# Attention of a Perceiver layer: eight TensorE runs per group become six, with seven rotating PSUM banks

## The chip, the cores and the metric

The kernel runs on one core of a Trainium2 chip. The metric is the device time of one launch in microseconds (us); a smaller number is better. The core has five engines that run side by side and wait for each other through semaphores: TensorE (PE in the profile; PEld is its loading of weights), VectorE (DVE), ScalarE (ACT), GpSimd (POOL) and SyncE (SP), which here issues most DMAs. TensorE writes its results to PSUM, which has eight banks, each of 512 float32 values on 128 partitions. The other memory on the core is SBUF.

## The reference

The layer has three parts, each added to the residual x of 16 batches, 64 rows and 1024 features, in float32. The change is to the first, cross attention:

```python
xq = layernorm(x).reshape(b, s, 8, 4, 32)      # 8 groups of 4 heads, 32 wide, 64 rows
xk = xv = ctx.reshape(b, 1601, 8, 32)          # keys and values are the same 1601 rows
scores = einsum("bsgrd,btgd->bgrst", xq, xk) / sqrt(32) + mask
out = einsum("bgrst,btgd->bsgrd", softmax(scores), xv)
x = x + out
```

The second part is a gated feed-forward layer (1024 to 2752) that zeroes the smaller half of its activations in each row; the third is a mixture of eight small experts of which each row uses two. The mask is one table of 64 x 1601 numbers that all batches share.

## The kernel before

**Groups.** Attention is cut into 64 groups: a batch, one half (`h`) of the eight key-value heads, and one half (`rh`) of the four query heads that share each of them. A group holds four key-value heads `g`, each with 2 x 64 = 128 rows of queries, so its scores are four tables of 128 x 1601.

**What one group goes through** (class `Group`, lines 235 to 358):

- `scores(c)`: TensorE multiplies queries and keys. The contraction is 32 long, so four heads occupy four strips of 32 rows of the array and run at once. The 1601 keys are cut into four parts (`PARTS`, line 29) of 289, 512, 288 and 512. One call is one part of all four heads: four matmuls, which show as eight rows, since float32 takes two passes. The 512 parts are called long here, the others short.
- `masked(c)`: VectorE reads each head's part from PSUM, adds the mask, writes it to SBUF (`sc`) and keeps the row maximum (`mx`). After the last part it reduces the maxima to `nm`.
- `softmax(g)`: ScalarE takes the exponential of one head's 1601 columns in place and sums it.
- `turn(heads)`: TensorE transposes two heads' exponentials in blocks of 128 columns, 26 transposes, four to a PSUM bank: three banks for each head and one that holds the last 65 columns of both. Eight copies take them to SBUF (`pT`): the first five by ScalarE, the sixth and the two small ones by VectorE.
- `values(c0, c1)`: TensorE multiplies the transposed blocks with the values. Each output is 32 wide, so the four heads use four strips of 32 columns and run at once. All 13 blocks accumulate in one bank, `po`, in two calls of 6 and 7 blocks.
- `keep()`: ScalarE copies `po` to `oT`; VectorE takes the reciprocals of the sums. When all groups of two batches are done, `finish_tile` transposes `oT` back and GpSimd scales it and adds it to x.

**The order.** Every engine works off its instructions in the order in which the program lists them (`InOrder`, lines 85 to 98). The loop of lines 418 to 484 goes over the groups n; each turn has two halves d. TensorE's order in a half is: a long score run of group n+1; in some halves the turning of later queries (`turn_queries`) or of finished results (`finish_tile`); the transposes of two heads of group n; a short score run of group n+1 (d = 0) or n+2 (d = 1); half of the values of group n-1. So there are four runs in a half and eight in a group. VectorE's order is: four long masks, copies 6 to 8, four short masks, and in the second half the reciprocals. ScalarE's is: five copies, two exponentials, and in the second half the copy of `po`. Scores and masks are thus half a group ahead of the loop, and six calls of `scores` stand ahead of it (line 407).

**PSUM.** One bank is `po`'s (`ps_o`). Three are for scores of heads 0 to 2 (`ps_s`). Four rotate (`ps_t`) among the scores of head 3, the transposes and the turned queries and results. A tile that is given a bank waits until all that used the tile before it in that bank is done.

**DMA.** `load_kv(b)` loads keys and values of a batch on SP's queue; it is called from `scores(0)` of the second group of the batch before. For the first batch the keys come in the four `PARTS`, each with two copies of its mask columns, in twelve DMAs. GpSimd in the meantime prepares sums of the feed-forward weights, one piece in each turn of the loop (`sums_in`, `sums_made`, `sums_out`).

**After attention** the feed-forward and expert parts run in an order that a planner (class `Plan`) works out from written costs and ranks. The last group's values and `keep` are its first tasks (lines 1239 and 1240).

Of the kernel before, what the change touches and what calls it, by code (L numbers as in the profile page):

```python
# [9 lines left out]
F32 = mybir.dt.float32  # L10
# [6 lines left out]
ALU = mybir.AluOpType  # L17
AX = mybir.AxisListType
PSUM = bass.MemoryType.PSUM

P = 128
B, S, D = 16, 64, 1024
T, C = 1601, 256
HD = 32
NT = B * S // P
NTC = (T + P - 1) // P
TL = T - (NTC - 1) * P

PARTS = [(0, 289), (289, 801), (801, 1089), (1089, T)]
NCH = len(PARTS)  # L30
I = 2752
IC = 344
NIC = I // IC
# [21 lines left out]
def tile_perceiver_layer(  # L55
# [22 lines left out]
    ident = const.tile([P, P], F32, name="ident")  # L78
# [18 lines left out]
    pe, dve, act = InOrder(nc.tensor), InOrder(nc.vector), InOrder(nc.scalar)  # L97
# [43 lines left out]
    otp = new_pool(late, "oT", 2, "right")  # L141
    twp = new_pool(early, "tw", 3)
    xp = new_pool(late, "x", 3, "right")
    ps_s = new_pool(early, "ps_s", 1, "left", PSUM)
    ps_t = new_pool(early, "ps_t", 4, "right", PSUM)

# [41 lines left out]
    def load_kv(b):  # L188
        kT = [ktp.tile([P, T], F32, tag="kT", name=f"kT{b}_{h}") for h in range(2)]
        v = [vp.tile([P, NTC, P], F32, tag="v", name=f"v{b}_{h}") for h in range(2)]  # L190
        full = (NTC - 1) * P
        for h in range(2):
            rows = ctx_t[b, h * P : (h + 1) * P]
            if b == h == 0:
                for t0, t1 in PARTS:
                    cols = slice(t0, t1)
                    sp_queue.dma_start(kT[h][:, cols], rows[:, cols])
                    for half in range(2):
                        sp_queue.dma_start(
                            mask2[half * S : (half + 1) * S, cols], mask[:, cols]  # L200
                        )
            else:
                sp_queue.dma_start(kT[h], rows)
        for h in range(2):
            cols = ctx_v[b, :, h * P : (h + 1) * P]
            sp_queue.dma_start(
                v[h][:, : NTC - 1, :], cols[:full].rearrange("(c p) d -> p c d", p=P)
            )
            sp_queue.dma_start(v[h][:TL, NTC - 1, :], cols[full:])
        kv[b] = kT, v  # L210
# [24 lines left out]
    class Group:  # L235
# [4 lines left out]
            self.name = f"{b}_{h}_{rh}"  # L240
            self.sc, self.pT = {}, {}

        def scores(self, c, spare=False):


            b, h, rh = self.b, self.h, self.rh
            if c == 0:
# [8 lines left out]
            t0, t1 = PARTS[c]  # L256
            homes = [[(ps_s, f"ps{g}"), (ps_t, "pt")] for g in range(3)]
            homes.append([(ps_t, "pt"), (ps_o, "po")])
            self.ps = []
            for g in range(4):  # L260
                home, tag = homes[g][spare]
                ps = home.tile([P, 512], F32, tag=tag, name=f"ps{g}_{self.name}_{c}")
                self.ps.append(ps)
            for g in range(4):
                rows = slice(g * HD, (g + 1) * HD)
                q = qT[b // 2][rows, h, b % 2, 2 * rh : 2 * rh + 2, :]
                pe.matmul(
                    self.ps[g][:, : t1 - t0],
                    q.rearrange("p r s -> p (r s)"),
                    kv[b][0][h][rows, t0:t1],  # L270
                    start=True,
                    stop=True,
                )

        def masked(self, c, heads=range(4)):


            t0, t1 = PARTS[c]
            for g in heads:
                dve.tensor_tensor_reduce(  # L280
                    out=self.sc[g][:, t0:t1],
                    in0=self.ps[g][:, : t1 - t0],
                    in1=mask2[:, t0:t1],
                    scale=1.0,
                    scalar=LOWEST,
                    op0=ALU.add,
                    op1=ALU.max,
                    accum_out=self.mx[:, g, c : c + 1],
                )
            if c == NCH - 1 and 2 in heads:  # L290
# [32 lines left out]
                )  # L323
            return copies

        def values(self, c0, c1):


            if c0 == 0:
                self.po = ps_o.tile([P, 512], F32, tag="po", name=f"po_{self.name}")  # L330
                self.po = self.po[:, :P]
            po, v = self.po, kv[self.b][1][self.h]
            for c in range(c0, c1):
                w = min(P, T - c * P)
                for g in range(4):
                    pe.matmul(
                        po[g * HD : (g + 1) * HD, :],
                        v[:w, c, g * HD : (g + 1) * HD],
                        self.pT[g][:w, c, :],
                        start=(c == 0),  # L340
                        stop=(c == NTC - 1),
                    )

        def keep(self):

            i, bb = self.b // 2, self.b % 2
            if bb == 0 and self.h == 0 and self.rh == 0:
                oT[i] = otp.tile([P, 2, 4, 2, S], F32, tag="oT", name=f"oT{i}")
                rs_tok[i] = small.tile([P, 2, 4, 4], F32, tag="rs", name=f"rs{i}")
            act.copy(  # L350
                oT[i][:, self.h, 2 * self.rh : 2 * self.rh + 2, bb, :],
                self.po.rearrange("p (r s) -> p r s", r=2),
            )
            for rl in range(2):
                dve.reciprocal(
                    rs_tok[i][bb * S : (bb + 1) * S, self.h, 2 * self.rh + rl, :],
                    self.sums[rl * S : (rl + 1) * S, :],
                )
# [35 lines left out]
    ng = len(groups)  # L394
# [9 lines left out]
        pe.transpose(warm[:, 0, :], ident, ident)  # L404
    for h in range(2):
        turn_queries(0, xn, h)
    for group, c in [(groups[0], c) for c in range(NCH)] + [(groups[1], c) for c in range(2)]:
        group.scores(c, spare=c % 2 == 1)
        if c % 2 == 0:
            for _ in range(4):  # L410
                pe.transpose(group.ps[3][:, 3 * P :], ident, ident)
        group.masked(c)
    for g in range(2):
        groups[0].softmax(g)

# [2 lines left out]
    for n in range(ng):  # L418
# [10 lines left out]
                sp_queue.dma_start(x[j], xs[j])  # L429
        for d in range(2):  # L430
            add = None
            long = (groups[n + 1], 2 * d + 1) if n + 1 < ng and n + d > 0 else None
            short = (groups[n + 1 + d], 2 - 2 * d) if n + 1 + d < ng else None
            if long:
                long[0].scores(long[1])
            if i < NT and d == 1 and m >= 6:
                turn_queries(i, xn, m - 6)
            if n > 8 and 3 <= 2 * m + d <= 4:
                copy, add = finish_tile(i - 2, 1 - d)
                act.copy(*copy)  # L440
            copies = group.turn((2 * d, 2 * d + 1))
            on_act = 3 if last else 5
            for copy in copies[:on_act]:
                act.copy(*copy)
            if long:
                long[0].masked(long[1], (3, 0, 1, 2))
            for copy in copies[on_act:]:
                dve.tensor_copy(*copy)
            if short:
                short[0].scores(short[1])  # L450
                short[0].masked(short[1])
            if d == 0:
                for g in (2, 3):
                    group.softmax(g)
            elif n + 1 < ng:
                for g in range(2):
                    groups[n + 1].softmax(g)
            if add:
                add()
            if n > 0:  # L460
                groups[n - 1].values(*((0, NTC // 2), (NTC // 2, NTC))[d])
                if d == 1:
                    groups[n - 1].keep()
            if i < NT:
                if (m, d) == (4, 0):
                    norm = Norm(x[i], f"q{i}")
# [769 lines left out]
    rank = {name: 10 + 10 * j for j, name in enumerate(order)}  # L1236
    gated = [gate(pairs[0], 0, rank["g0"], lambda i: [])]

    t = add("PE", 2.9, lambda: groups[-1].values(0, NTC), [], rank["g0"] - 5)
    t = add("ACT", 0.3, lambda: groups[-1].keep(), [t], 0)  # L1240

    def end():
        for h in range(2):
# [172 lines left out]
```

## Time and profile before

The median of three runs is 1718.9 us (1718.66 to 1722.92). The profiled execution has a span of 1719.5 us, 0.6 above the median.

| What | Value |
|---|---|
| Median of the runs | 1718.9 us |
| Profiled execution, first to last instruction | 1719.5 us |
| Busy over the span: TensorE, VectorE, ScalarE, GpSimd | 99%, 82%, 73%, 32% |
| Attention, to the end of the last values | 842 us |
| Mean time of one long mask, one short mask | 0.69, 0.45 us |
| One copy of a transposed bank: ScalarE, VectorE | 0.61, 0.69 us |
| One exponential of 128 x 1601 | 1.67 us |
| Granted TensorE clock | 0.995 of full speed |

A row of the timeline gives start, duration, engine, operation and the tiles written and read, with the number of instructions merged into it; the bracket is the idle time of the engine before it and what ended it. `ps` are scores in PSUM, `pt` transposed blocks in PSUM, `pT` the same in SBUF, `po` values, `sc` scores and exponentials in SBUF. A row of stretches gives the window, its length, then for PE, PEld, DVE, ACT and POOL the busy time and instructions, the granted clock, the share of the DMA engines and GB/s. Matmul rows overlap each other and their ends are modelled, so the start of the first weight load of one run to that of the next is used as the length of a run. Most instructions show line 93, that of a helper; the tiles tell them apart.

### The profile page before, as it was taken

The page shows a single profiled execution, that of the slowest core. Times are in us where ns is not written, and L with a number is a line of the kernel's source. Part 1 is how long each engine was busy: PE and PEld are TensorE (multiplying, and loading weights), DVE is VectorE, ACT ScalarE, POOL GpSimd, SP SyncE. Part 2 cuts the span into 40 slices and gives each one's busy share as a digit, 9 for nine tenths or more (in the row PEclk, how much of TensorE's full clock was granted, in tenths as well). Part 3 has the DMA queues.
Part 4 walks back from the last instruction along what each step waited for, and adds up shares of the span by engine and source line. Part 5 has one row for each costly group of instructions (what it writes and reads, how often), then busy time and mean ns, then how long its engine had stood idle before and what let it go on. Part 6 is the DMA issues. An engine that isn't in the chain of part 4 may idle for free. (4 is left out here: it accounts for less than half of the span.)

```text
span 1719.5 us, 38732 instructions
## 1 busy us (share of the span) xinstructions
PE 1694.0 (99%) x15102; PEld 1152.2 (67%) x15102; DVE 1413.0 (82%) x3655; ACT 1259.6 (73%) x1780; POOL 557.2 (32%) x584
## 2 busy tenths in 40 slices
PE   8999999999999999999999999999989999999999
PEld 6777777777777777777766666655645646645644
DVE  7888888888888888888627999999999989999703
ACT  5999999999999999999544676577657782778010
POOL 2045454454444454110120211222282013331631
PEclk9999999999999999999999999999999999999999
DMA  8246456555556646121499999988969978888984
GB/s 248 74 122 207 148 194 210 188 166 195 170 185 206 204 159 208 57 75 58 182 349 324 308 292 304 302 267 291 324 202 292 309 251 301 283 294 270 316 265 143
DMA packets 132327, 384.56 MB, mean 224 GB/s; under 512 B 9489, under 2 KB 61233, under 8 KB 132145
## 3 DMA queue, kind: packets, MB, share of 16 engines
q1 hardware_dynamic: 113280, 312.83, 55.5%
q0 software_dynamic: 18432, 68.16, 12.1%
q8 instruction: 120, 1.97, 0.5%
q10 hardware_dynamic: 432, 1.09, 0.2%
q14 instruction: 63, 0.51, 0.1%
HBM read 339.58 MB, written 42.47 MB: 222 GB/s over the span
## 5 line engine op out<-in xcount | busy, mean ns | idle before, releaser
L93 DVE CUSTOM_DVE_ANT_0 sc<-ps,mask 128x512 f32<-128x512 f32 (+2 forms) x1024 | 526.4, 571 | 104.8 <-PE ps L93 104.4
L93 ACT ACTIVATE sign<-a,cand 128x2752 int8<-128x2752 f32 x136 | 351.9, 2587 | 110.9 <-DVE cand L93 110.5
L93 ACT ACTIVATE sc<-sc,nm 128x1601 f32<-128x1601 f32 x256 | 420.2, 1667 | 11.5 <-DVE nm L93 11.5
L93 PEld LDWEIGHTS pt<-ident,sc 128*128 128x128 f32 (+1 forms) x3328 | 361.9, 141 | 77.3 <-issue 72.8
L93 PE MATMUL pt<-ident,sc 128*128 128x128 f32 (+1 forms) x3328 | 391.1, 274 | 1.0 <-ACT sc L93 0.9
L93 DVE TENSOR_SCALAR_CACHE_REDUCE junk<-a,cand 128x2752 uint8<-128x2752 f32 x124 | 381.7, 3078 | 4.0
L93 ACT COPY pT<-pt 128x512 f32<-128x512 f32 x636 | 323.9, 609 | 46.5 <-PE pt L93 46.2
L93 PE MATMUL pg_g<-w_g,hS 128*128 128x344 f32 x896 | 261.2, 453 | 2.6 <-DMA w_g<-ts 1.8
L93 PE MATMUL pg_u<-w_u,hS 128*128 128x344 f32 x896 | 263.4, 452 | 0.0
L93 POOL TENSOR_TENSOR tw<-tw 128x344 f32<-128x344 f32 (+1 forms) x192 | 175.9, 927 | 265.5 <-DMA tw<-in_wg_dram 87.3
L93 PE MATMUL ps<-kT,qt 32*128 32x512 f32 (+2 forms) x2048 | 248.1, 550 | 4.6 <-DMA kT<-in_ctx_t_dram 3.4
L93 PE MATMUL pd<-w_d,s 128*128 128x512 f32 x528 | 235.2, 599 | 0.0
L93 PEld LDWEIGHTS pg_g<-w_g,hS 128*128 128x128 f32 x896 | 169.5, 190 | 91.0 <-issue 3.3
L93 PEld LDWEIGHTS pg_u<-w_u,hS 128*128 128x128 f32 x896 | 168.8, 190 | 87.4 <-issue 3.4
L93 PE MATMUL po<-pT,v 128*32 128x128 f32 x6656 | 208.2, 274 | 0.4 <-ACT oT L93 0.4
L93 PEld LDWEIGHTS po<-pT,v 128*32 128x32 f32 x6656 | 174.1, 110 | 48.6 <-issue 45.7
L93 PEld LDWEIGHTS pd<-w_d,s 128*128 128x128 f32 x528 | 99.9, 193 | 115.7 <-issue 114.6
L93 DVE COPY pT<-pt 65x128 f32<-65x128 f32 (+1 forms) x388 | 141.0, 418 | 22.9 <-PE pt L93 16.0
L93 PEld LDWEIGHTS ps<-kT,qt 32*128 32x128 f32 x2048 | 83.3, 184 | 53.9 <-DVE mx L93 36.7
L93 ACT ACTIVATE s<-s 128x344 f32<-128x344 f32 (+1 forms) x70 | 36.6, 535 | 74.8 <-DVE s L93 74.7
L93 POOL TENSOR_TENSOR s<-s,rank 128x688 f32<-128x688 f32 x32 | 62.4, 1965 | 77.3 <-DVE rank L93 76.7
L93 DVE DVE_READ_ACCUMULATOR2_ANT mx<- 128x1 f32 x1024 | 84.0, 82 | 0.0
(322 smaller groups left out, 1216.6 us busy)
## 6 DMA issues: line engine op xcount, KB each, us to landing
w_g<-ts SPq DMA_DIRECT2D x64, 688.0 KB
w_u<-ts SPq DMA_DIRECT2D x64, 688.0 KB
w_d<-ts SPq DMA_DIRECT2D x48, 768.0 KB
w_g<-in_wg_dram SPq DMA_DIRECT2D x48, 688.0 KB
w_u<-in_wu_dram SPq DMA_DIRECT2D x48, 688.0 KB
w_d<-in_wd_dram SPq DMA_DIRECT2D x36, 768.0 KB
kT<-in_ctx_t_dram SPq DMA_DIRECT2D x31, 800.5 KB
v<-in_ctx_v_dram SPq DMA_DIRECT2D x32, 768.0 KB
```

Of the source, the lines that this page charges most:

```text
L93: return tc.keep_in_program_order(getattr(self.engine, op)(*args, **kwargs))
```

## The change

The keys are cut into two halves (801 and 800), and each half into a part of 512 and one of 289 or 288. `scores(d)` now computes all four heads' scores of a half in one run: eight matmuls, first the four long parts, then the four short ones. Seven of them take banks of `ps_t`, which now has seven banks and serves scores, transposes and turned queries and results; `ps_s` is gone. The eighth goes to the first columns of the remaining bank, `shared`, whose last 128 columns are `po`.

TensorE's order in a half becomes: scores of half d of group n+1; half of the values of group n-1; turned queries or results where there are any; transposes of two heads of group n. That is three runs in a half and six in a group. VectorE's is: eight masks, (second half: the maximum), the copy of `po`, (second half: the reciprocals), the copies of transposed blocks. Scores are no longer half a group ahead; only those of the first group stand ahead of the loop.

The values of a group are two partial sums: the first half's is copied from `po` to `oT`, the second half's is added there, both by VectorE (before: one copy by ScalarE). In halves with turned queries or results ScalarE takes one of the eight copies less and VectorE one more. The first batch's keys and mask come in three pieces, nine DMAs. `load_kv` of the next batch is called from `scores(0)` half a turn later. In the planner's tasks, the last group's `keep` moves from ScalarE to VectorE and its reciprocals become a task of their own.

```diff
-PARTS = [(0, 289), (289, 801), (801, 1089), (1089, T)]
-NCH = len(PARTS)
+HALVES = [(0, 801), (801, T)]
+BANK = 512
+LOADS = [(0, 512), (512, 801), (801, T)]
+NCH = 4
...
-    ps_s = new_pool(early, "ps_s", 1, "left", PSUM)
-    ps_t = new_pool(early, "ps_t", 4, "right", PSUM)
+    ps_t = new_pool(early, "ps_t", 7, "left", PSUM)
+    shared = ps_o.tile([P, 512], F32, tag="po", name="shared")
+    po = shared[:, 3 * P :]
...
-        def scores(self, c, spare=False):
+        def scores(self, d):
...
+            t0, t1 = HALVES[d]
+            mid = t0 + BANK
+            self.parts = []
+            for j in range(8):
+                g, (c0, c1) = j % 4, ((t0, mid), (mid, t1))[j // 4]
+                bank = shared
+                if j < 7:
+                    bank = ps_t.tile([P, BANK], F32, tag="pt", name=f"ps{j}_{self.name}_{d}")
+                ps = bank[:, : c1 - c0]
                 rows = slice(g * HD, (g + 1) * HD)
...
+                self.parts.append((g, c0, c1, ps, 2 * d + j // 4))
+
+        def masked(self, d):
...
+            for g, t0, t1, ps, c in self.parts:
...
-        def values(self, c0, c1):
...
+        def values(self, d):
+            c0, c1 = ((0, NTC // 2), (NTC // 2, NTC), (0, NTC))[d]
...
-                        start=(c == 0),
-                        stop=(c == NTC - 1),
+                        start=(c == c0),
+                        stop=(c == c1 - 1),
...
-            act.copy(
-                oT[i][:, self.h, 2 * self.rh : 2 * self.rh + 2, bb, :],
-                self.po.rearrange("p (r s) -> p r s", r=2),
-            )
+            rows = oT[i][:, self.h, 2 * self.rh : 2 * self.rh + 2, bb, :]
+            new = po.rearrange("p (r s) -> p r s", r=2)
+            if d == 1:
+                dve.tensor_tensor(rows, new, rows, ALU.add)
+            else:
+                dve.tensor_copy(rows, new)
+
+        def inverse(self):
...
-    for group, c in [(groups[0], c) for c in range(NCH)] + [(groups[1], c) for c in range(2)]:
-        group.scores(c, spare=c % 2 == 1)
...
+    for d in range(2):
+        groups[0].scores(d)
+        for _ in range(4):
+            pe.transpose(po, ident, ident)
+        groups[0].masked(d)
...
-            long = (groups[n + 1], 2 * d + 1) if n + 1 < ng and n + d > 0 else None
-            short = (groups[n + 1 + d], 2 - 2 * d) if n + 1 + d < ng else None
-            if long:
-                long[0].scores(long[1])
+            following = groups[n + 1] if not last else None
+            if following:
+                following.scores(d)
+            if n > 0:
+                groups[n - 1].values(d)
+            if following:
+                following.masked(d)
+            if n > 0:
+                groups[n - 1].keep(d)
+                if d == 1:
+                    groups[n - 1].inverse()
+            on_act = 3 if last else 5
             if i < NT and d == 1 and m >= 6:
                 turn_queries(i, xn, m - 6)
+                on_act -= 1
             if n > 8 and 3 <= 2 * m + d <= 4:
                 copy, add = finish_tile(i - 2, 1 - d)
                 act.copy(*copy)
+                on_act -= 1
             copies = group.turn((2 * d, 2 * d + 1))
-            on_act = 3 if last else 5
             for copy in copies[:on_act]:
                 act.copy(*copy)
-            if long:
-                long[0].masked(long[1], (3, 0, 1, 2))
             for copy in copies[on_act:]:
                 dve.tensor_copy(*copy)
-            if short:
-                short[0].scores(short[1])
-                short[0].masked(short[1])
...
-            if n > 0:
-                groups[n - 1].values(*((0, NTC // 2), (NTC // 2, NTC))[d])
-                if d == 1:
-                    groups[n - 1].keep()
...
-    t = add("PE", 2.9, lambda: groups[-1].values(0, NTC), [], rank["g0"] - 5)
-    t = add("ACT", 0.3, lambda: groups[-1].keep(), [t], 0)
+    t = add("PE", 2.9, lambda: groups[-1].values(2), [], rank["g0"] - 5)
+    t = add("DVE", 0.3, lambda: groups[-1].keep(2), [t], 0)
+    t = add("DVE", 0.4, lambda: groups[-1].inverse(), [t], 0)
```

More of the change, by code (lines that the diff above doesn't have):

```diff
@@ L194, in load_kv @@
             if b == h == 0:
-                for t0, t1 in PARTS:
+                for t0, t1 in LOADS:
                     cols = slice(t0, t1)
@@ L241, in __init__ @@
             self.sc, self.pT = {}, {}
-        def scores(self, c, spare=False):
+        def scores(self, d):
             b, h, rh = self.b, self.h, self.rh
-            if c == 0:
+            if d == 0:
                 self.sc = [
@@ L255, in scores @@
                     load_kv(b + 1)
[L256 to L264, printed above, removed]
+            t0, t1 = HALVES[d]
[7 more added lines that the diff above has]
+                ps = bank[:, : c1 - c0]
                 rows = slice(g * HD, (g + 1) * HD)
@@ L267, in scores @@
                 pe.matmul(
-                    self.ps[g][:, : t1 - t0],
+                    ps,
                     q.rearrange("p r s -> p (r s)"),
-                    kv[b][0][h][rows, t0:t1],
+                    kv[b][0][h][rows, c0:c1],
                     start=True,
@@ L273, in scores @@
                 )
-        def masked(self, c, heads=range(4)):
-            t0, t1 = PARTS[c]
-            for g in heads:
+                self.parts.append((g, c0, c1, ps, 2 * d + j // 4))
+        def masked(self, d):
+            for g, t0, t1, ps, c in self.parts:
                 dve.tensor_tensor_reduce(
                     out=self.sc[g][:, t0:t1],
-                    in0=self.ps[g][:, : t1 - t0],
+                    in0=ps,
                     in1=mask2[:, t0:t1],
@@ L289, in masked @@
                 )
-            if c == NCH - 1 and 2 in heads:
+            if d == 1:
                 self.nm = small.tile([P, 4], F32, tag="nm", name=f"nm_{self.name}")
@@ L324, in turn @@
             return copies
-        def values(self, c0, c1):
[L329 to L332, printed above, removed]
+        def values(self, d):
+            c0, c1 = ((0, NTC // 2), (NTC // 2, NTC), (0, NTC))[d]
+            v = kv[self.b][1][self.h]
             for c in range(c0, c1):
@@ L339, in values, with keep @@
                         self.pT[g][:w, c, :],
-                        start=(c == 0),
-                        stop=(c == NTC - 1),
+                        start=(c == c0),
+                        stop=(c == c1 - 1),
                     )
-        def keep(self):
+        def keep(self, d):
             i, bb = self.b // 2, self.b % 2
-            if bb == 0 and self.h == 0 and self.rh == 0:
+            if bb == 0 and self.h == 0 and self.rh == 0 and d != 1:
                 oT[i] = otp.tile([P, 2, 4, 2, S], F32, tag="oT", name=f"oT{i}")
                 rs_tok[i] = small.tile([P, 2, 4, 4], F32, tag="rs", name=f"rs{i}")
-            act.copy(
-                oT[i][:, self.h, 2 * self.rh : 2 * self.rh + 2, bb, :],
-                self.po.rearrange("p (r s) -> p r s", r=2),
-            )
+            rows = oT[i][:, self.h, 2 * self.rh : 2 * self.rh + 2, bb, :]
[5 more added lines that the diff above has]
+        def inverse(self):
+            i, bb = self.b // 2, self.b % 2
             for rl in range(2):
@@ L406, in tile_perceiver_layer @@
         turn_queries(0, xn, h)
-    for group, c in [(groups[0], c) for c in range(NCH)] + [(groups[1], c) for c in range(2)]:
-        group.scores(c, spare=c % 2 == 1)
[L409 to L412, printed above, removed]
+    for d in range(2):
[3 more added lines that the diff above has]
+        groups[0].masked(d)
     for g in range(2):
@@ L431, in tile_perceiver_layer @@
             add = None
-            long = (groups[n + 1], 2 * d + 1) if n + 1 < ng and n + d > 0 else None
-            short = (groups[n + 1 + d], 2 - 2 * d) if n + 1 + d < ng else None
-            if long:
-                long[0].scores(long[1])
+            following = groups[n + 1] if not last else None
[7 more added lines that the diff above has]
+                groups[n - 1].keep(d)
+                if d == 1:
+                    groups[n - 1].inverse()
+            on_act = 3 if last else 5
             if i < NT and d == 1 and m >= 6:
                 turn_queries(i, xn, m - 6)
+                on_act -= 1
             if n > 8 and 3 <= 2 * m + d <= 4:
@@ L440, in tile_perceiver_layer @@
                 act.copy(*copy)
+                on_act -= 1
             copies = group.turn((2 * d, 2 * d + 1))
-            on_act = 3 if last else 5
             for copy in copies[:on_act]:
                 act.copy(*copy)
-            if long:
-                long[0].masked(long[1], (3, 0, 1, 2))
             for copy in copies[on_act:]:
                 dve.tensor_copy(*copy)
-            if short:
-                short[0].scores(short[1])
-                short[0].masked(short[1])
[L452 to L457, printed above, removed]
+            for g in range(2):
+                if d == 0:
+                    group.softmax(2 + g)
+                elif following:
+                    following.softmax(g)
             if add:
                 add()
-            if n > 0:
-                groups[n - 1].values(*((0, NTC // 2), (NTC // 2, NTC))[d])
-                if d == 1:
-                    groups[n - 1].keep()
             if i < NT:
```

## The prediction

> **What bounds the kernel now.** I read the page first, then the stretches, then the weight loads and VectorE in order of time in one group, and last the start of the kernel.
>
> ```profile
> span 1719.5 us, 38732 instructions
> PE 1694.0 (99%) x15102; PEld 1152.2 (67%) x15102; DVE 1413.0 (82%) x3655; ACT 1259.6 (73%) x1780; POOL 557.2 (32%) x584
> ```
> ```profile
> 50.00:450.00 400.00, 400.00 (x5942) 305.54 (x5940) 339.61 (x1297) 371.17 (x607) 173.98 (x188) 1.00 0.53 172
> ```
> In attention (to 842 us) TensorE is busy all the time at clock 1.00, VectorE 85% and ScalarE 93%. Matmul rows overlap, so I take run lengths from one weight load to the next, here for one half group and the start of the next:
>
> ```profile
> 405.12 0.31 PEld L93 LDWEIGHTS ps<-kT,qt 32*128 32x128 f32 x8 [0.20 <-DVE mx L93]
> 406.19 2.82 PEld L93 LDWEIGHTS pt<-ident,sc 128*128 128x128 f32 x26 [0.76 <-issue]
> 409.18 0.31 PEld L93 LDWEIGHTS ps<-kT,qt 32*128 32x128 f32 x8 [0.17 <-DVE mx L93]
> 409.88 1.25 PEld L93 LDWEIGHTS po<-pT,v 128*32 128x32 f32 x48 [0.39 <-issue]
> 411.33 0.31 PEld L93 LDWEIGHTS ps<-kT,qt 32*128 32x128 f32 x8 [0.20 <-DVE mx L93]
> ```
> Long scores 1.07, transposes 2.99, short scores 0.70, values 1.45: 6.21 us. The other half has 56 value matmuls, 1.67 long: 6.43. The idle times in brackets recur alike in every group: runs draining, no late partner. TensorE's order of runs is the bound.
>
> ```profile
> 406.41 0.69 DVE L93 CUSTOM_DVE_ANT_0 sc<-ps,mask 128x512 f32<-128x512 f32 x1 [0.36 <-PE ps L93]
> 409.07 1.08 DVE L93 COPY pT<-pt 128x512 f32<-128x512 f32 x3
> 410.08 0.45 DVE L93 CUSTOM_DVE_ANT_0 sc<-ps,mask 128x288 f32<-128x288 f32 x1
> ```
> VectorE's first mask starts 1.29 after the long run's start. Its three copies start 2.88 after the transposes' start and end at 410.15, 0.97 after the next score run has begun. Today nothing on TensorE waits for them: the short run has three banks of its own.
>
> ```profile
> 9.17 0.31 PEld L93 LDWEIGHTS ps<-kT,qt 32*128 32x128 f32 x8 [0.17 <-issue]
> 9.71 0.92 PEld L93 LDWEIGHTS ps<-kT,qt 32*128 32x128 f32 x8 [0.22 <-DVE mx L93]
> 11.01 0.20 PEld L93 LDWEIGHTS ps<-ident 128*128 128x128 f32 x2 [0.39 <-issue]
> ```
> ```profile
> 9.95 0.18 PEld L93 LDWEIGHTS ps<-kT,qt 32*128 32x128 f32 x1
> ```
> ```profile
> 10.20 0.08 DVE L93 DVE_READ_ACCUMULATOR2_ANT mx<- 128x1 f32 x1
> ```
> ```profile
> 10.33 0.18 PEld L93 LDWEIGHTS ps<-kT,qt 32*128 32x128 f32 x1
> ```
> The start holds, once, what the change makes the rule: a long and a short score run without a switch between. It took 1.84 (9.17 to 11.01), no less than apart (1.77), because its last two banks were late: one load at 9.95, the last at 10.33, just after VectorE's mask that frees the bank ends at 10.28.
>
> **The run saved.** Matmul passes in that stretch start at 9.17, 9.71, 10.14 and, for the heads not delayed, 10.38; a short run's second pass is followed by the next run 0.35 later. Undelayed it is 0.53 + 0.43 + 0.25 + 0.35 = 1.56 against 1.07 + 0.70 = 1.77: 0.21 saved per half (a fill and a drain). Fitting long and short runs by their columns gives 0.22. There are 63 x 2 = 126 halves with scores: -26.5 us.
>
> **Values straight into transposes.** This switch does not occur cleanly before. Bounds: the fixed part of a score run, 0.22, more or less per half (a loss to +27 us, a gain to -27). I take 0, since the switches that do occur all leave the same gap: the last transpose starts at 422.06 and streams 0.11, the next load is at 422.26; the last value matmul at 424.20, the next load at 424.40: 0.09 each.
>
> **The new wait.** The merged run needs seven banks, the transposes before it used the same seven. The seventh transposed bank holds both 65-row pieces, copied last, by VectorE, 0.97 after the new run's start; the weight load that waits follows some 0.05 later (10.28 to 10.33 above): 1.02. What lateness costs, from the startup run: a load at 9.95 (0.78 in) cost nothing, one at 10.33 (1.16 in) made the run 1.84 - 1.56 = 0.28 longer, so cost begins at 0.88, and 1.02 costs about 0.15. Bounds 0 (if it hides like the load 0.78 in) and 0.28; I take 0.15, since 1.02 lies between the two rows. Queued behind it on TensorE: the eighth scores, values, transposes. 124 halves (the first two wait for exponentials anyway): +18.6.
>
> **Whether VectorE is on time.** From the start of a score run: first mask at 1.29; four long masks 0.61 apart, four short 0.38 apart, last read: 5.32. In the first half the copy of partial values follows; nearest row, a copy of as many columns (65x128), 0.20 apart; furthest, 128x512, 0.61. Free at 5.55 (5.96). It is wanted 2.88 into the transposes: 1.56 + 0.15 + 1.45 + 2.88 = 6.04. On time either way. In the second half come the maximum (0.10), the added partial (nearest 0.20; furthest, the 128x344 add, 0.51) and two reciprocals, now ahead of the copies (0.37): 6.04 (6.35), wanted at 6.26. On time by 0.2, or 0.09 late: up to +6. I take the near rows. Two bn_stats (0.68) per eight groups delay the next masks by 0.2, inside this slack.
> The transposes in turn take over the banks of the scores: they start at 3.16, the fourth bank opens at 4.5 and the seventh at 5.8; their masks have been read by 3.8 and 5.0. Hidden by VectorE's lead of 0.7; without it each 0.1 late is 0.1 on TensorE.
>
> **A copy moved to VectorE.** In 28 halves with queries turned or a tile finished, one 128x512 copy leaves ScalarE. In such halves transposes take 3.04 (412.79 to 415.83) and the copy of the sixth bank could start at 2.93, the fifth's one bank (0.44) earlier. Four copies then end 2.49 + 0.61 + 0.61 + 0.20 + 0.28 = 4.19 in: 1.15 into the next run instead of 0.97, +0.17 each: +4.8. Bounds 0 and 0.61 (the whole copy).
>
> **ScalarE** loses the 0.29 us copy of values. Its half is five copies and two exponentials, 2.38 + 3.24 + 0.23 = 5.85, below 6.1: hidden behind TensorE; were TensorE quicker than 5.85, ScalarE would be next.
>
> **DMAs and queues.** The next batch's four loads are emitted one half later, past a store of x on SP's queue. In the trace SP sits in those issues 19 to 27 us at a time until buffers come free, and keys are used two groups or more after landing: nothing. POOL's own queue keeps its order. At the start nine loads replace twelve, of the same bytes; the last 289 columns now come with 801. Four more masks (1.5) precede the first exponential, but the first half then needs no more work: about +0.3, bounds -0.5 and +2. At the end, the second values of the group before last fill a wait for exponentials that ended at 828.5 and 833.7 and no longer delay the last values at 839.1: -1.4 (0 to -1.9). Past 842 us two small tasks stand on VectorE in the planned order where one stood on ScalarE; if that reorders neighbours, I bound it by three of the POOL tasks of 1.3 to 1.6 us beside it, 4 us either way, and take 0.
>
> **Sum.** -26.5 + 18.6 + 4.8 + 0.3 - 1.4 = -4.2, on a profiled span of 1719.5 that is 0.6 above the median: 1719.5 - 4.2 = 1715.3, less 0.6, 1715.
>
> **A rule against the change.** The row first: each bank now has one writer and one reader at a time, and no wait of values for masks stands in the trace.
> The Trainium skill (PSUM — Partial Sum Buffer, Terms) says that two engines must not use the same bank and partitions at once. The eighth scores share a bank with the values, so by that rule one must wait. Were it the values, until the eighth mask at 5.3 instead of 1.6, an estimate from it is 3.7 x 126 = +466 us. The new program order puts the values ahead of the masks, so VectorE would wait instead, and values end near 3.4, before it needs that bank at 4.9: the sum holds 0. No run shown here decides it.
>
> **Rivals.**
> 1. The bank wait hides (the copies' release is early enough, as with the load at 9.95). For: 0.78 in cost nothing. Against: 1.02 is past the 0.88 where cost began. Price: -18.6, and the 28 shifted copies cost half: 1694 or so.
> 2. Slower: VectorE falls behind. The wait grows one for one with VectorE's lateness. From 0.21 mean wait per half nothing is gained; from 0.26 it is 0.3% slower. For: it is busy nearly 5.9 of 6.2 us, in order. Against: 0.2 of slack on the near rows. At 0.1 us late in all 126 halves: +12.6, about 1728.
> 3. The merged run does not save its 0.21, because values into transposes drains longer than I took. 0.1 per half gives the same 1728; the full 0.21, about 1741.
>
> **How the numbers follow.** Likeliest, a wait of 0.12 to 0.2: 0.47, own range 1709 to 1721. Rival 1: 0.24. Rival 2: 0.19. Rival 3: 0.10. About 0.3% (5 us) is what a measurement here can tell from no change: 1713.7 and 1724.1 are the limits. Of the likeliest, 0.17 lies below, 0.27 within, 0.03 above; rival 1 all faster; rivals 2 and 3 give 0.05 within and 0.24 above. Faster 0.41, same 0.32, slower 0.27. Range 1696 to 1731.
>
> **What would show it.** Right: in each half one score run of sixteen matmul rows, its last two heads loaded about 1.0 after the first, with idle put down to a DVE copy of pT; 1.71 from that run to the values; 1.45 or 1.67 from the values to the transposes; halves of 6.15 and 6.37 instead of 6.21 and 6.43; VectorE idle before its pT copies. Rival 1 shows runs of 1.56; rival 2 no such VectorE idle and loads later than 1.1; rival 3 values that hold the array longer than 1.45 and 1.67. The whole reading is wrong if transposes wait for masks, or for ScalarE's exponentials.

## The result and the profile after

The changed kernel is slower: a median of 1730.8 us (1729.44 to 1731.66, four runs) against 1718.97 (1718.66 to 1722.92, four runs beside it), a ratio of 1.0057 [1.0042, 1.0071]. The forecast was 1715. The time is still inside the range of 1696 to 1731, at its edge, and on the other side of no change.

The page of the kernel after, its span and its engines (busy us, share of the span, instructions):

```profile
span 1728.4 us, 38747 instructions
PE 1702.1 (98%) x15098; PEld 1209.6 (70%) x15098; DVE 1455.9 (84%) x3810; ACT 1236.4 (72%) x1688; POOL 561.0 (32%) x584
```

The same stretch of attention as before, as window, length, the busy times of PE, PEld, DVE, ACT and POOL, clock, DMA share and GB/s:

```profile
50.00:450.00 400.00, 400.00 (x5869) 330.69 (x5868) 356.69 (x1360) 355.38 (x558) 173.40 (x186) 1.00 0.52 172
```

The spans differ by 8.9 us (1728.4 - 1719.5), the medians by 11.8. The rest is the execution that was profiled: the listed runs take 1.8 us more than their spans, so that of before would have taken 1721.3, some 2.3 more than its median, and that of after took 1730.19, 0.6 less than its median. What follows explains the 8.9. TensorE stays at clock 1.00 and busy throughout, but with 73 fewer matmul rows in these 400 us (5869 against 5942). VectorE took over 17 us of work and ScalarE lost 16.

One half group on TensorE's weight loads (start, duration, engine, line, operation, tiles, count, idle before and what ended it):

```profile
404.70 0.31 PEld L95 LDWEIGHTS ps<-kT,qt 32*128 32x128 f32 x8 [0.17 <-ACT pT L95]
405.24 0.28 PEld L95 LDWEIGHTS ps<-kT,qt 32*128 32x128 f32 x2 [0.22 <-ACT pT L95]
405.66 0.30 PEld L95 LDWEIGHTS ps<-kT,qt 32*128 32x128 f32 x3
405.82 0.18 PEld L95 LDWEIGHTS shared<-kT,qt 32*128 32x128 f32 x1
405.89 0.18 PEld L95 LDWEIGHTS ps<-kT,qt 32*128 32x128 f32 x1
405.93 0.18 PEld L95 LDWEIGHTS shared<-kT,qt 32*128 32x128 f32 x1
406.50 1.25 PEld L95 LDWEIGHTS shared<-pT,v 128*32 128x32 f32 x48 [0.39 <-issue]
407.95 2.82 PEld L95 LDWEIGHTS pt<-ident,sc 128*128 128x128 f32 x26 [0.20 <-issue]
410.94 0.31 PEld L95 LDWEIGHTS ps<-kT,qt 32*128 32x128 f32 x8 [0.17 <-ACT pT L95]
```

Three runs in place of four: scores 1.80 (404.70 to 406.50), values 1.45, transposes 2.99, together 6.24; before it was 6.21. From 40 to 800 us, the score run is 1.80 or 1.81 in 89 of 117 halves, and 1.96 or 1.97 in the 28 that follow a half with turned queries or results. Forecast were 1.71 and 1.88.

VectorE around it, in the same columns:

```profile
404.59 1.08 DVE L95 COPY pT<-pt 128x512 f32<-128x512 f32 x3
...
406.02 0.68 DVE L95 CUSTOM_DVE_ANT_0 sc<-ps,mask 128x512 f32<-128x512 f32 x1
...
409.97 0.28 DVE L95 COPY oT<-shared 128x128 f32<-128x128 f32 x1
410.83 1.08 DVE L95 COPY pT<-pt 128x512 f32<-128x512 f32 x3 [0.57 <-PE pt L95]
```

The copies of transposed blocks (one of 128x512 and the two small ones) start 2.88 after the transposes (407.95 to 410.83), and VectorE was idle for 0.57 before them: it is on time. In the run shown first they end at 405.67, 0.97 into it. Both are as forecast. Over 60 to 830 us the waits (us in all, times, longest), of the kernel after and then of the kernel before, say the same: VectorE now waits for transposed blocks, and hardly for scores any more, for which it waited before:

```profile
DVE pT L95 <- PE pt L95: 66.8, 112, 0.9
...
DVE sc L95 <- PE ps L95: 13.0, 70, 0.2
```

```profile
DVE sc L93 <- PE ps L93: 95.6, 120, 1.0
...
DVE pT L93 <- PE pt L93: 11.8, 29, 0.6
```

**The mis-sized wait.** The trace's single records give what the merged lines hide. The loads are numbered here by the run's eight matmuls, the four long ones first; each shows twice, once for each pass. VectorE's last copy, then the first pass of the seventh load:

```profile
405.39 0.28 DVE L95 COPY pT<-pt 65x128 f32<-65x128 f32 x1
```

```profile
405.79 0.18 PEld L95 LDWEIGHTS ps<-kT,qt 32*128 32x128 f32 x1
```

The copy ends at 405.671. The seventh load starts at 405.787, 1.09 into the run and 0.12 after the copies' end, where I had taken 0.05. Between the two stands an instruction of TensorE's sequencer alone, an EVENT_SEMAPHORE, from 405.711 to 405.762. The eighth load, into `shared`, follows at 405.823: 1.125 into the run. By the rule drawn from the start of the kernel before (cost begins at 0.88; 0.881 unrounded) the later of these loads costs 1.125 - 0.881 = 0.244, and 1.56 + 0.244 = 1.804 is what a half shows.

The Trainium skill (Perfetto Trace Analysis, Identifying Dependency Chains) says that an instruction that waits for several engines may have EventSemaphore instructions put ahead of it. The trace agrees: the row stands ahead of the load into the bank of the small pieces, and it moves with that bank, to the eighth load where banks seven and eight are exchanged and to the fifth where the small pieces come in the middle. The page gives no price.

**After attention.** The lag behind the kernel before, read at the same instruction of both:

| Point (time in the kernel before) | Lag |
|---|---|
| third run of transposes (34.49) | -2.0 |
| end of the last values (842.09) | +5.4 |
| first gate product of the feed-forward (846.75) | +5.9 |
| gate products at 881 | +10.5 |
| last products of the feed-forward (1705.5) | +8.7 |

At the start the kernel before waits for a DMA of keys, ahead of the last scores of the first group:

```profile
15.06 3.05 PE L93 MATMUL ps<-kT,qt 32*128 32x512 f32 x16 [3.40 <-DMA kT<-in_ctx_t_dram]
```

In the kernel after, these scores start loading at 10.20 and wait for no DMA. Whether this is all of the 2.0, no run tells.

Some 4.6 us go at one place, between 847 and 881. SP's queue of the kernel before, and then of the kernel after (start, duration, queue, line, what is issued):

```profile
826.55 0.32 SPq L551 DMA_DIRECT2D w_g<-ts  x1
826.96 0.86 SPq L551 DMA_DIRECT2D w_g<-in_wg_dram  x2
827.87 1.28 SPq L551 DMA_DIRECT2D w_g<-ts  x2
829.19 0.44 SPq L551 DMA_DIRECT2D w_g<-in_wg_dram  x1
852.10 0.32 SPq L1247 DMA_DIRECT2D xs<-x  x1
```

```profile
832.11 0.32 SPq L556 DMA_DIRECT2D w_g<-ts  x1
832.53 1.26 SPq L556 DMA_DIRECT2D w_g<-in_wg_dram  x2
833.84 1.11 SPq L556 DMA_DIRECT2D w_g<-ts  x2
857.99 0.32 SPq L1253 DMA_DIRECT2D xs<-x  x1
858.36 0.43 SPq L556 DMA_DIRECT2D w_g<-in_wg_dram  x1
```

Before, six loads of gate weights are issued and then the last store of x. After, five; the sixth stands behind the store, which waits for finished results until 857.99, and so is issued 29 us later. TensorE's idle time before gate products (us in all, times, longest) grows by 3.9 of these, from 843 to 890 us of the kernel before, then from 843 to 900 us of the kernel after:

```profile
PEld pg_g L93 <- issue: 2.4, 1, 2.4
```

```profile
PEld pg_g L95 <- issue: 6.3, 9, 4.4
```

What put the store ahead of the sixth load in the program, no run tells.

### The profile page after: what moved, and what is told of

Same layout as the page of the kernel before. It is cut to its first block, busy times and chain, and to the rows that moved or that the text cites. A ratio compares the mean times of both kernels' runs of the same rounds, so it can differ in the third digit from the quotient of the medians.

```text
span 1728.4 us, 38747 instructions
## 1 busy us (share of the span) xinstructions
PE 1702.1 (98%) x15098; PEld 1209.6 (70%) x15098; DVE 1455.9 (84%) x3810; ACT 1236.4 (72%) x1688; POOL 561.0 (32%) x584
## 3 DMA queue, kind: packets, MB, share of 16 engines
q8 instruction: 120, 1.97, 0.5%
q10 hardware_dynamic: 432, 1.09, 0.2%
## 5 line engine op out<-in xcount | busy, mean ns | idle before, releaser
L95 DVE CUSTOM_DVE_ANT_0 sc<-ps,mask 128x512 f32<-128x512 f32 (+2 forms) x896 | 468.3, 588 | 16.9 <-PE ps L95 16.1
L95 ACT COPY pT<-pt 128x512 f32<-128x512 f32 x608 | 310.3, 606 | 68.9 <-PE pt L95 68.6
L95 PE MATMUL ps<-kT,qt 32*128 32x512 f32 (+2 forms) x1792 | 242.4, 543 | 0.1
L95 DVE COPY pT<-pt 65x128 f32<-65x128 f32 (+1 forms) x416 | 157.7, 436 | 74.7 <-PE pt L95 74.2
L95 PE MATMUL shared<-pT,v 128*32 128x128 f32 x6656 | 208.5, 274 | 0.7 <-DVE pT L95 0.7
L95 PEld LDWEIGHTS shared<-pT,v 128*32 128x32 f32 x6656 | 174.2, 110 | 49.4 <-issue 45.1
L95 PEld LDWEIGHTS ps<-kT,qt 32*128 32x128 f32 x1792 | 134.9, 183 | 71.1 <-ACT pT L95 41.8
L95 PE MATMUL shared<-kT,qt 32*128 32x289 f32 (+1 forms) x256 | 95.7, 453 | 0.0
```

The lines of the kernel that those rows point to most:

```text
L95: return tc.keep_in_program_order(getattr(self.engine, op)(*args, **kwargs))
```

## The experiments

Each edit is made on the changed kernel. Beside these runs the kernel before took 1722.4 us, against 1718.97 beside the changed kernel, so versions are compared by their ratios to it. The theory: the merged run does save its 0.21, and all it loses is the lateness of its last load past 0.88. The main rival: a merged run is itself longer than I took, whatever the banks do.

**The small pieces in the middle.** The bank with both 65-row pieces is filled and copied between the full ones, so that the score run meets it earlier, and VectorE copies no extra bank.

```diff
-            for g, c0, c1 in parts + [(g, NTC - 1, NTC) for g in heads]:
+            for g, c0, c1 in parts[:4] + [(g, NTC - 1, NTC) for g in heads] + parts[4:]:
...
-            return copies
+            return [copies[j] for j in (0, 1, 2, 3, 6, 4, 5, 7)]
...
                 turn_queries(i, xn, m - 6)
-                on_act -= 1
...
                 act.copy(*copy)
-                on_act -= 1
```

> The two 65-row pieces are transposed in the middle of a transpose run, after the fourth bank, and VectorE copies them ahead of the last full bank; ScalarE takes five copies in every half. Theory A (the changed kernel loses because the seventh bank of a merged score run is freed late, by VectorE's last copy): the last bank is now free some 0.80 to 0.90 us after the score run's start instead of 0.97, without the second wait that goes with the small bank, so the late load comes at 0.85 to 0.95 instead of 1.09 and costs 0 to 0.07; score runs of 1.56 to 1.63 us instead of 1.80 (1.96 in the 28 halves with a moved copy), time 1696 to 1705 us. Rival B (eight matmuls in one run take 1.80 by themselves, whatever the banks): runs stay at 1.80, and only the moved copies' 4.5 us go: about 1726 us.

Measured: 1697.69 us (1694.99 to 1700.17) against 1722.38 for the kernel before, ratio 0.986 [0.9845, 0.9875]. Weight loads of one score run, then VectorE's two copies that belong to it:

```profile
408.23 0.31 PEld L95 LDWEIGHTS ps<-kT,qt 32*128 32x128 f32 x8 [0.17 <-ACT pT L95]
408.77 0.50 PEld L95 LDWEIGHTS ps<-kT,qt 32*128 32x128 f32 x3 [0.22 <-issue]
409.09 0.18 PEld L95 LDWEIGHTS shared<-kT,qt 32*128 32x128 f32 x1
409.20 0.20 PEld L95 LDWEIGHTS ps<-kT,qt 32*128 32x128 f32 x3
409.22 0.18 PEld L95 LDWEIGHTS shared<-kT,qt 32*128 32x128 f32 x1
409.79 1.47 PEld L95 LDWEIGHTS shared<-pT,v 128*32 128x32 f32 x56 [0.39 <-issue]
```

```profile
407.76 0.28 DVE L95 COPY pT<-pt 65x128 f32<-65x128 f32 x1
408.34 0.69 DVE L95 COPY pT<-pt 128x512 f32<-128x512 f32 x1 [0.30 <-PE pt L95]
```

The run is 1.56 (408.23 to 409.79), in 102 of 118 halves between 60 and 800 us. VectorE's last copy now ends 0.80 in and the last load is at 409.089, 0.86 in, just inside the 0.88. The extra semaphore row stands ahead of the fifth load and is done before the run begins (408.096 to 408.147), so it is off the path. With the same seven banks and the same runs, the order in which the banks come free is worth 0.24 in each half (the moved copies alone, in the experiment after next, change 28 halves only). In this 0.24 is what the semaphore row had cost; no run moves it alone. The merged run saves what the start of the kernel before promised; the rival falls.

Of the other 16 runs, nine are 1.60 to 1.68. Seven are 1.74, all after the second half of one turn in eight: a bn_stats just before that half, and the reciprocals in it, make VectorE late, now that a half is shorter.

**The same, with ScalarE on the last full bank.**

```diff
-            return [copies[j] for j in (0, 1, 2, 3, 6, 4, 5, 7)]
+            return [copies[j] for j in (0, 1, 2, 3, 7, 4, 5, 6)]
```

> As the other kernel with the pieces in the middle, but ScalarE copies the last full bank and VectorE the one before it. Theory A: the last bank is free some 0.72 after the score run's start and the load comes before 0.88: runs of 1.56, time about 1696 us; if ScalarE, which now waits for the end of the transposes before its exponentials, becomes the bound, up to 1704. Rival B: runs of 1.80, about 1726 us.

Measured: 1699.14 (1697.84 to 1700.22), ratio 0.9868 [0.9854, 0.9883]; runs of 1.56 in 103 of 119 halves between 60 and 800 us. The intervals of the two overlap: which engine frees the last bank matters little, if the order is right.

**Only the moved copies undone.** Both lines `on_act -= 1` go, and nothing else.

> Only the moved copy is undone: ScalarE takes five copies also in the 28 halves with turned queries or results. Theory A: their score runs fall from 1.96 to 1.80, 28 x 0.16 = -4.5 us on the changed kernel: about 1726 us; ScalarE has room for it (6.4 of 6.8 us). Rival C (ScalarE is the bound in those halves): transposes wait for exponentials and the time stays at 1731 us or rises.

Measured: 1725.35 (1724.27 to 1728.55), ratio 1.0022 [1.0011, 1.0033], apart from the 1.0042 to 1.0071 of the changed kernel; every score run between 40 and 800 us is 1.80 or 1.81. The 28 runs of 1.96 are the moved copy, 0.16 each, 4.5 us in all. The kernel is still slower than before: the wait in the other halves alone uses up the gain.

**One copy more on VectorE in every half.**

```diff
-            on_act = 3 if last else 5
+            on_act = 3 if last else 4
...
-                on_act -= 1
...
-                on_act -= 1
```

> The wait made longer: ScalarE takes four of the eight copies in every half, VectorE four. Theory A: the seventh bank is free 1.15 after the run's start everywhere, the runs are 1.96 in all halves (now in 28 of 126), so 98 x 0.16 = +15.7 us on the changed kernel: about 1746 us. Rival B: runs stay at 1.80 in the 98 halves and the time at about 1731 us.

Measured: 1751.59 (1750.51 to 1754.47), ratio 1.0177 [1.016, 1.0194]. Of 114 score runs between 40 and 800 us, 100 are 1.96 or 1.97 and 14 are 2.12 to 2.38. One run of each kind, on the weight loads:

```profile
408.05 0.31 PEld L95 LDWEIGHTS ps<-kT,qt 32*128 32x128 f32 x8 [0.17 <-ACT pT L95]
...
410.01 1.47 PEld L95 LDWEIGHTS shared<-pT,v 128*32 128x32 f32 x56 [0.39 <-issue]
...
414.67 0.31 PEld L95 LDWEIGHTS ps<-kT,qt 32*128 32x128 f32 x8 [0.17 <-ACT pT L95]
415.28 0.18 PEld L95 LDWEIGHTS ps<-kT,qt 32*128 32x128 f32 x1 [0.30 <-DVE pT L95]
...
417.04 1.25 PEld L95 LDWEIGHTS shared<-pT,v 128*32 128x32 f32 x48 [0.39 <-issue]
```

The first is 1.96; in the second, 2.37, already the fifth load (415.28) stands behind a copy of VectorE. So a later copy costs its lateness in every half. In the 14 long runs, seven longer by 0.16 and seven by 0.41, VectorE falls behind as well; they cost 4 us together, which the expected 1746 us left out. With them the runs add 15.7 + 4 = 19.7 to the changed kernel; the profiled spans differ by 1749.6 - 1728.4 = 21.2.

**The seventh and eighth matmuls exchange banks.** The load of the late bank then comes last, and none stands behind it.

```diff
-                if j < 7:
+                if j != 6:
```

> The changed kernel with one swap: the seventh matmul of a score run takes the bank it shares with the values, and the eighth takes the seventh rotating bank, so only one load stands behind the late bank instead of two. Theory A: the load still comes 1.09 after the run's start, but the second one 0.036 later is gone: runs 1.76 to 1.77 instead of 1.80 (1.92 to 1.93 instead of 1.96), 126 x 0.036 = -4.5 us: about 1726 us. Rival (the cost of a late bank does not go by its lateness but is a fixed 0.24): runs stay at 1.80, about 1731 us.

Measured: 1728.56 (1725.91 to 1729.84), ratio 1.0038 [1.0023, 1.0053]. Score runs are 1.77, and 1.93 in the 28: 0.035 less than after. The start of one run, its eighth load (both passes) and the next values:

```profile
409.85 0.31 PEld L95 LDWEIGHTS ps<-kT,qt 32*128 32x128 f32 x8 [0.17 <-ACT pT L95]
...
410.94 0.29 PEld L95 LDWEIGHTS ps<-kT,qt 32*128 32x128 f32 x2
411.62 1.47 PEld L95 LDWEIGHTS shared<-pT,v 128*32 128x32 f32 x56 [0.39 <-issue]
```

The eighth load starts 1.09 in, so the rule gives 1.56 + 1.09 - 0.88 = 1.77. The intervals of the ratios (1.0023 to 1.0053 here, 1.0042 to 1.0071 after) overlap; the lengths of the runs decide.

**The last values.** In the changed kernel the last group's values take 4.07 instead of 2.98 before, with 0.96 of waiting for VectorE's five copies of the last half. These stand behind a normalization of x (`xn_f`), as before, and now also behind the added partial values and two reciprocals, and start at 843.75. Here ScalarE keeps five copies in the last half, on top of the first experiment.

```diff
-            on_act = 3 if last else 5
+            on_act = 5 if not last else 3 + 2 * d
```

> The kernel with the pieces in the middle, and in the last half of the last group ScalarE takes five copies instead of three, so VectorE, which is busy with the norm of the next part, takes three. Theory: the last values, 4.07 us long now because they wait 0.96 for VectorE's copies, take about 3.0 again: -1 us, 1696.7 us against 1697.7. Rival: another wait takes its place and the time stays.

Measured: 1696.9 (1695.07 to 1697.65), ratio 0.9854 [0.984, 0.9869], no different from the first experiment. On TensorE's loads the last values are one run, and the feed-forward's first transposes follow 3.05 later:

```profile
810.66 2.85 PEld L95 LDWEIGHTS shared<-pT,v 128*32 128x32 f32 x104 [0.33 <-DVE oT L95]
813.71 0.86 PEld L95 LDWEIGHTS pt_f<-ident,xn_f 128*128 128x128 f32 x8 [0.20 <-issue]
```

Attention ends 0.8 sooner than in the first experiment (813.7 against 814.5), and nothing of it reaches the gate products at 881: both kernels are 23.0 ahead of the kernel before there. They wait for the late sixth weight load.

**The store off SP's queue.** On top of the first experiment, the last store of x goes to GpSimd's queue.

```diff
-        nc.sync.dma_start(xs[NT - 1], x[NT - 1])
+        nc.gpsimd.dma_start(xs[NT - 1], x[NT - 1])
```

> The kernel with the pieces in the middle, and one DMA moved: the store of the last finished tile of x goes by GpSimd's queue instead of SP's, where it now stands before the sixth weight load of the feed-forward part (in the kernel before, after it). Theory D (4 of the us that the changed kernel loses after attention come from that load being issued behind the store): the sixth load is issued with the first five, the gap of about 4 us in the first gate product goes, and 2 to 4 us of it reach the end: 1693.5 to 1696 us against 1697.7. Rival: the load waits for its buffer, not for the queue: no difference, 1697.7.

Measured: 1695.02 (1694.44 to 1697.55), ratio 0.9848 [0.9833, 0.9863]. SP's queue of this kernel:

```profile
799.89 1.33 SPq L554 DMA_DIRECT2D w_g<-in_wg_dram  x2
801.27 1.04 SPq L554 DMA_DIRECT2D w_g<-ts  x2
802.35 0.43 SPq L554 DMA_DIRECT2D w_g<-in_wg_dram  x1
805.78 23.50 SPq L737 DMA_DIRECT2D s<-xs  x4
```

The sixth load is issued with the others, and the lead over the kernel before holds: 26.95 at the first gate product, 26.5 at 881 and 26.95 at the last products of the feed-forward, where the first experiment has 27.0, 23.0 and 25.0. So in the first experiment the loss between these points is that order in SP's queue: some 4 us where it occurs and 1.9 at the last products. These are two profiled executions; the ratios alone would not show it, since their intervals overlap. In the changed kernel itself, which loses 4.6 us between the first gate product and 881, no run moved the store.

**All together.** The order of the first experiment, the store on GpSimd's queue, ScalarE's five copies in the last half, and the reciprocals behind VectorE's copies.

```diff
                 groups[n - 1].keep(d)
-                if d == 1:
-                    groups[n - 1].inverse()
...
                 dve.tensor_copy(*copy)
+            if n > 0 and d == 1:
+                groups[n - 1].inverse()
```

> All of it together: pieces in the middle, five copies on ScalarE always, the store on GpSimd's queue, the last copies on ScalarE, and the two reciprocals behind the copies on VectorE, which gives VectorE back 0.37 us in every second half (seven of its score runs took 1.74 instead of 1.56 after the statistics of a norm). Theory A: those seven and the seven of 1.62 fall to 1.56, -1.6 us; with the two others 1692 to 1695 us, 1.6% below the kernel before. If the parts overlap, 1697.

Measured: 1690.88 us (1688.8 to 1692.44) against 1722.4, ratio 0.9819 [0.9803, 0.9835], 1.1 us under the range expected. The page:

```profile
span 1689.3 us, 38748 instructions
...
PE 1667.1 (99%) x15098; PEld 1178.4 (70%) x15098; DVE 1439.9 (85%) x3780; ACT 1250.5 (74%) x1718; POOL 558.1 (33%) x585
```

Score runs are 1.56 in 117 of 118 halves between 60 and 800 us: with the reciprocals out of the way, the runs of 1.74 are gone. The lead is 29.9 at the first gate product and 30.5 at the last products of the feed-forward. TensorE has the instructions of the changed kernel, in the same three runs to a half, and is busy for 35 us less. This version beats both kernels.

## Why the prediction was wrong

Its sum beside what the traces show, in us of the span:

| Step | Predicted | Measured |
|---|---|---|
| The run saved, 126 halves | -26.5 | -26.5 (1.77 to 1.56, first experiment) |
| The new wait, 124 halves | +18.6 | +30.3 (0.244 each) |
| A copy moved to VectorE, 28 halves | +4.8 | +4.5 (0.16 each) |
| Start | +0.3 | -2.0 |
| End of attention | -1.4 | -0.9 (what is left to +5.4) |
| After attention | 0 | +3.5 (+5.4 to +8.9) |
| Sum | -4.2 | +8.9 |

- **The step that failed is "The new wait".** Its mechanism was right: VectorE's copies end 0.97 into the run, cost begins at 0.88, and lateness beyond that costs one for one. Its size was not: 30.3 us measured for 18.6. "The weight load that waits follows some 0.05 later" was read from a load that waits for one bank's mask; here the load follows 0.12 later, and the eighth behind it 0.036 later still, which sets the end of the run. The cost is 0.244, not 0.15. The prediction's own break-even was a mean wait of 0.21; with the moved copies the mean is 0.28. The 11.7 us that were missed turn the result: with a wait of 0.15 and all else as measured, the span would have been 2.8 shorter, not 8.9 longer. I had put 0.15 between two rows and never asked which of the two late loads ends the run.
- **Values straight into transposes** was right at 0: values stay 1.45 and 1.67, transposes 2.99 and 3.04. Rival 3 is out.
- **Whether VectorE is on time** was right for the changed kernel: it is idle before its copies, so rival 2 is out, though the kernel landed where rival 2's price was. In the faster versions its slack is gone: the first experiment has seven halves where it is late.
- **A copy moved to VectorE** was right, 0.16 for 0.17.
- **Rival 1**, a wait that hides, did not happen here; the first experiment makes it happen by the order of the banks. Its price, 1694, is near that kernel's ratio of 0.986, which is 1695 on 1718.97.
- **Start**: the first transposes come 2.5 us earlier (19.23 for 21.69, both put down to the first exponentials), outside the bounds of -0.5 and +2. The wait of 3.40 for keys, which the kernel before has there and the kernel after has not, stood in no term; no run tells whether the nine loads in place of twelve removed it.
- **End of attention**: the gain of 1.4 was partly undone by the last values, 1.1 longer, which wait for VectorE's copies behind the added partial values and the reciprocals. That wait was not in the sum.
- **After attention** was bounded at 4 us either way by tasks of VectorE and GpSimd. The bound held (+3.5), the cause did not: I had looked at two engines and not at where a store falls among SP's loads.
- **The shared bank**: values do not wait for the eighth masks, so the 0 held against the 466 us estimated from the Trainium skill (PSUM — Partial Sum Buffer, Terms); the waits of TensorE show no such entry.

The Trainium skill (Perfetto Trace Analysis, Optimization Strategy) says that a gap repeating on the engine that should be saturated can mean too few buffers. The gap of 0.24 repeats in every half here; the first experiment closes it with the same seven banks, so here their number was enough, and the order of their release made the gap.

## What to carry to other kernels

When two runs on the bounding engine are merged over the same rotating buffers, each buffer must come free earlier relative to the new run. Write down when every one is released and when the run takes it, then let the one that is finished last be taken last, and give the short pieces to an early place. Here this order decided between 0.2% slower and 1.4% faster, both with five copies on ScalarE, and without an instruction more on any of the compute engines. Look also at what each DMA queue holds at the border to the next phase, where a load can come to stand behind a store that waits.

## What was not expected of the hardware

- One rule fits nearly every merged score run between 60 and 800 us: its length is 1.56 plus what the start of its eighth load (first pass) exceeds 0.881. Loads at 0.86, 1.09, 1.125 and 1.286 give 1.56, 1.77, 1.80 and 1.965; 1.16, at the start of the kernel before, gives the 1.84 from which the rule was drawn. The exception is one run of 1.68 in each version with the small pieces in the middle: its eighth load is in time, but the sixth load is late, and its second pass comes last. What fits that one too is the last of the sixteen rows: in all of these runs the next run's first load follows its start by 0.57.
- A load ahead of which an EVENT_SEMAPHORE row stands started 0.12 after the copy that freed its bank, where a load without one started 0.05 after: some 0.07 for the second wait, an estimate from these two of 8 us over 124 halves when it lies on the path.
